# A layered convolution-attention kernel on one core: the state sum folded by transfers, d and du repeated inside SBUF, the c norm's moments on ScalarE, and new step tables

## The chip, the cores and the metric

The kernel runs on one core of a Trainium2 chip. Its engines are PE (TensorE, matrix products into PSUM), DVE (VectorE), ACT (ScalarE), POOL (GpSimd) and SP (SyncE, which here only issues transfers); 16 DMA engines move data between DRAM and SBUF, and inside SBUF. Each engine works through its own instructions in order and waits on semaphores for the others. The metric is the device time of one execution in microseconds (us): the median of three runs of the kernel before is 1173.12 us (1171.61 to 1173.38).

## The reference, cut to what matters

The input `x` is 4 images of 64 x 64 points with 96 channels, in float32: 4 x 4096 tokens of 96.

Layer 0 normalizes x over groups of 3 channels (group norm), then each token over its 96 channels (here: the c norm), projects it to `value`, `gate`, `delta` and to A, B and C of 96 channels x 16 states each, and runs a recurrence along the 4096 tokens of an image:

```python
h_new = d * (A_t * h) + d * (B_t * u_t[..., None])     # 96 channels x 16 states
y = g_t * jnp.sum(C_t * h_new, axis=-1)                # sum over the 16 states
```

`y @ W_out + b_out` is added to x. Layer 1 normalizes the tokens (the a norm), applies an attention without softmax, with 6 heads, whose products can be taken in another order (a Gram matrix of the tokens of one image, then one 97 x 96 matrix for the whole image), adds it to the tokens, normalizes again (the f norm) and adds a two-layer network with 384 hidden units, whose operands are rounded to 8 bits and whose sums are rounded to 16.

## The kernel before

**Tiles and chunks.** An image is cut into 8 chunks of 512 tokens, 32 chunks in all. The 96 x 16 states are cut into 12 tiles of 128 rows: 4 groups of 4 states (`sh`) times 3 groups of 32 channels (`cg`). One tile of one chunk is one *step* of the main loop: 384 steps, 12 to a chunk. In step s, PE makes B of tile s+3, A of tile s+1 and C of tile s, each as three matrix products that together keep float32 precision; ACT copies B from PSUM and adds its bias (`b_copy`, L888); POOL multiplies it by du (`b_mul`, L891); DVE multiplies A by d in PSUM (`a_mul`, L900), runs the recurrence over the 512 tokens as a scan (`scan`, L907), and multiplies h by C (`c_mul`, L931). In four of the twelve tiles, listed in `ON_POOL`, this last product is made by ACT and POOL in two parts (`c_copy`, L937, and `c_mul_pool`, L940). ACT keeps the last column of h for the next chunk (`keep`, L917). B has one PSUM bank, A two, C two, and three ("M") serve everything else.

**The state sum.** The products of one chunk lie in four tiles `ch` of 128 x 3 x 512, one for each `sh`. POOL issues three accumulating transfers (`gather`, L946) that add the tiles of `sh` 1, 2 and 3 to that of `sh` 0. In it, the 128 rows are four states times 32 channels. `state_sum` (L955) adds the four on PE by a product with `fold`, four stacked unit matrices, into PSUM. `gated` (L993) multiplies by the gate, and `project_out` (L998) and `residual` (L1003) follow.

**The front of a chunk** (class `Front`) runs 9 to 39 steps ahead of the chunk: load, `centre` and `scale` for the group norm on POOL (L747, L750), `stats` of the c norm on DVE, `rstd` on POOL, `apply` on ACT, the transposition, the split into two parts (`low` and three transfers of SP), and the projections for d and u. d and d*u come as `dd` of 96 x 2 x 512. Every tile needs them repeated over its four states: `write` (L824) puts `dd` into DRAM and `read` (L831) brings it back four times into `rep`, 32 rows each.

**The norms.** `LayerNorm.stats` runs `bn_stats` (L433) and `bn_aggr` (L435) on DVE, four of each. `Roots.root` then runs four small instructions on POOL: variance plus epsilon (L406), the power -1/2 (L409), the mean times -1 (L412), times the root (L413). `apply` (L450) scales and shifts on ACT.

**The order.** It is written out by hand: the table `AT` gives, for each piece of work, the step in relation to its chunk's (or its image's) first step, and `at` puts it on that step's list, which runs after the step's own instructions. So a piece's number says what it stands behind on each engine's queue, and on SP's. What does not fit into the 384 steps goes to a planner (`end`, class `Plan`) with costs and ranks, which tries 1500 random orders by its own costs and takes the best. The start, up to step 6, is planned in the same way (`planned_start`). In images 1 to 3 the loop carries the second layer of the image before as well.

Of the kernel before, what the change touches and what calls it, by code (L numbers as in the profile page):

```python
# [9 lines left out]
F32 = mybir.dt.float32  # L10
# [7 lines left out]
P = 128  # L18
# [4 lines left out]
J = 4  # L23
# [17 lines left out]

    "load_x": -39, "centre": -25, "scale": -24, "stats": -22, "rstd": -22, "apply": -21,
    "transpose": -14, "affine": -13, "upper": -13, "low": -12, "proj_d": -9, "d_out": -9,
    "proj_u": -9, "du_out": -9, "write": -9, "read": -6, "proj_gate": -3, "gate_out": -1,

    "gather1": 7, "gather2": 11, "gather3": 14,

    "state_sum": 18, "gated": 18, "project_out": 19, "residual": 19, "stats_a": 20,
    "rstd_a": 21, "apply_a": 22, "transpose_a": 33, "keep": 34, "spill": 39, "gram": 24,
    "gram_out": 24, "gram_add": 26,  # L50

    "fetch": 21, "attention": 26, "residual_f": 26, "stats_f": 26, "rstd_f": 27, "apply_f": 29,
    "transpose_f": 30, "quant_in": 31, "hidden0": 37, "relu0": 37, "hidden1": 31, "relu1": 33,
    "hidden2": 38, "relu2": 38, "project_f": 40, "round_out": 40, "bias_out": 40, "total": 46,
    "store": 51,

    "sums": -31, "sums_out": -30,
}
MV_BUFS = {1: 4, 2: 2}
END_RANKS = (-2, 0, 1)  # L60
END_PAIR = (0, 1, 1, 2, 2, 3, 3, 4)
APPLY_DVE = (0, 2, 4, 6, 7)
QUANT_POOL = (1, 4)
BIAS_DVE = (0, 1, 2, 3, 4, 5, 6, 7)
TOTAL_DVE = (1, 3, 5, 7)
ON_POOL = (0, 2, 7, 8)
XBUFS = 15
END_TRIES = 1500
# [3 lines left out]
def conv_attn_hybrid_kernel(  # L72
# [34 lines left out]
        "bu": 5, "h": 3, "cha": 2, "chb": 3,  # L107
# [97 lines left out]
    minus = const.tile([P, 3, J], F32, name="minus")  # L205
    nc.gpsimd.memset(minus, -1.0)
    eps_t = {}
    for eps, n in ((1e-3, 1), (1e-5, 2)):
        eps_t[eps] = const.tile([P, n, J], F32, name=f"eps{n}")
        nc.gpsimd.memset(eps_t[eps], eps)  # L210
# [169 lines left out]
    class Roots:  # L380
# [14 lines left out]
        def root(self, shift=True):  # L395
            if self.done:
                return
            self.done = True
            n = len(self.of)
            for k, ln in enumerate(self.of):  # L400
                if k and ln.eps == self.of[k - 1].eps:
                    continue
                m = k + 1
                while m < n and self.of[m].eps == ln.eps:
                    m += 1
                nc.gpsimd.tensor_tensor(  # L406
                    self.r[:, k:m], self.mv[:, k:m, :, 1], eps_t[ln.eps][:, 0 : m - k], ALU.add
                )
            nc.gpsimd.tensor_tensor(self.r, self.r, mhalf[:, 0:n], ALU.pow)  # L409
            if not shift:  # L410
                return
            nc.gpsimd.tensor_tensor(self.nmr, self.mv[:, :, :, 0], minus[:, 0:n], ALU.mult)  # L412
            nc.gpsimd.tensor_tensor(self.nmr, self.nmr, self.r, ALU.mult)  # L413

    class LayerNorm:
# [9 lines left out]
        def stats(self, src):  # L425
# [8 lines left out]
            for j in range(J):  # L434
                nc.vector.bn_aggr(self.mv[:, j, :], st[:, j, :])  # L435

# [3 lines left out]

        def offset(self):

            nc.vector.tensor_scalar(self.r, self.mv[:, :, 1], self.eps, None, ALU.add)

        def root(self):
            nc.gpsimd.tensor_tensor(self.r, self.r, mhalf[:, 0], ALU.pow)
# [19 lines left out]
    class Plan:  # L466
# [23 lines left out]
        def run(self, fill=None):  # L490
# [67 lines left out]
            rng = random.Random(1)  # L558
# [24 lines left out]
    steps = {}  # L583

# [151 lines left out]
    class Front:  # L736
# [15 lines left out]
        def stats(self):  # L752
            self.ln.stats(self.t)
# [53 lines left out]
        def wide_d(self, cg):  # L807
            if cg == 0:
                rep[self.b, self.i] = sb("rep", [P, 2, NCG, TC], F32, f"rep_{self.nm}")
# [782 lines left out]
```

## Time and profile before

| | before |
|---|---|
| median of three runs | 1173.12 us |
| the profiled execution's own time | 1169.27 us |
| its span | 1167.5 us |
| PE, DVE busy | 1129.6, 1116.8 us |
| POOL, ACT busy | 1008.9, 811.3 us |
| first scan, last scan start | 35.1, 1102.7 us |

A profile is of one execution. "Busy" is the time in which at least one instruction of the engine was under way; PE's ends are modelled. A row of a group has the source line, the engine, the operation, what it writes and reads, the shapes and the count, then the total busy time in us, the mean of one in ns, the idle time before them and what ended it. A row of waits has the waiting engine, line and result, what it waited for, the total in us, the times and the longest. In a row of a timeline stand the start, the duration, the engine, the line and the operation. In a row of a stretch stand the stretch, its length, busy us of PE, its weight loads, DVE, ACT and POOL (each with the number of instructions), the granted clock, the DMA share and GB/s.

### The profile page before, as it was taken

Reading aid. Unit: us, or ns where it says so; the run is one execution under the profiler, and the core shown is the slowest. Engines: PE = TensorE matmul, PEld = TensorE weight load, DVE = VectorE, ACT = ScalarE, POOL = GpSimd, SP = SyncE. Lnnn points to the kernel's source line nnn. Section 1 sums busy time; section 2 is a strip of 40 time slices with the busy share of each in tenths; the row PEclk is TensorE's granted clock in tenths of the full one; section 3 lists DMA queues with packets and bytes.
Section 4 is the critical chain, followed back from the end, with each engine's and each line's share of the span. In section 5 each row is a group of like instructions: output and inputs, shape, how many; then the busy total and the mean of one; then the engine's idle time right before and its main releaser. Section 6 shows DMA issues by size and latency. Waiting matters only on the chain. (4 is left out here: it accounts for less than half of the span.)

```text
span 1167.5 us, 19144 instructions
## 1 busy us (share of the span) xinstructions
PE 1129.6 (97%) x5868; PEld 865.4 (74%) x5868; DVE 1116.8 (96%) x2110; ACT 811.3 (69%) x1818; POOL 1008.9 (86%) x1166
## 2 busy tenths in 40 slices
PE   6999999999999999999999999999999999999984
PEld 5777776777777777777877777777777777777662
DVE  6999999999999999999999999999999999999986
ACT  4666656555556777777777777787777777776477
POOL 5798888888889899899999999999999999988643
PEclk7999999999999999999999999999999999999999
DMA  7577777787776777687777778667776876777321
GB/s 183 137 167 146 165 158 160 157 178 164 166 162 151 161 166 175 148 185 162 159 163 167 165 165 189 149 152 159 167 172 149 183 160 157 150 161 166 78 82 55
DMA packets 104289, 182.13 MB, mean 156 GB/s; under 512 B 42637, under 2 KB 50769, under 8 KB 104186
## 3 DMA queue, kind: packets, MB, share of 16 engines
q1 hardware_dynamic: 90060, 106.96, 38.9%
q0 software_dynamic: 13536, 73.93, 31.8%
q8 instruction: 46, 0.75, 0.3%
q14 instruction: 57, 0.47, 0.1%
q10 hardware_dynamic: 590, 0.02, 0.0%
HBM read 69.12 MB, written 24.77 MB: 80 GB/s over the span
## 5 line engine op out<-in xcount | busy, mean ns | idle before, releaser
L891 POOL TENSOR_TENSOR bu<-bu,rep 128x512 f32<-128x512 f32 x384 | 511.3, 1342 | 51.1 <-ACT state L917 39.7
L907 DVE TENSOR_TENSOR_SCAN h<-Aps,state,bu 128x512 f32<-128x512 f32 x336 | 426.1, 1268 | 0.3 <-issue 0.2
L888 ACT ACTIVATE bu<-Bps,b_bac 128x512 f32<-128x512 f32 x384 | 262.8, 684 | 198.7 <-PE Bps L283 190.8
L900 DVE SCALAR_TENSOR_TENSOR Aps<-Aps,b_bac,rep 128x512 f32<-128x512 f32 x384 | 281.8, 734 | 3.6 <-PE Aps L283 3.1
L283 PE MATMUL Bps<-xs,w 128*128 128x512 f32 x768 | 266.9, 429 | 3.4 <-ACT bu L888 3.1
L283 PE MATMUL Aps<-xs,w 128*128 128x512 f32 x768 | 241.7, 395 | 1.2 <-DVE h L907 1.0
L940 POOL TENSOR_TENSOR ch<-ch,h 128x512 f32<-128x512 f32 x126 | 168.1, 1334 | 9.7 <-ACT ch L937 5.1
L283 PEld LDWEIGHTS Aps<-xs,w 128*128 128x128 f32 x768 | 143.6, 188 | 37.2 <-DVE h L907 2.9
L283 PEld LDWEIGHTS Bps<-xs,w 128*128 128x128 f32 x768 | 126.5, 190 | 45.5 <-ACT gx_ps L632 12.6
L283 PE MATMUL Aps<-xl,w 128*128 128x512 f32 x384 | 151.8, 395 | 0.0
L283 PE MATMUL Bps<-xl,w 128*128 128x512 f32 x384 | 151.4, 394 | 0.0
L283 PE MATMUL Cps<-xs,w 128*128 128x512 f32 x384 | 120.6, 395 | 0.0
L283 PE MATMUL Dps<-xs,w 128*128 128x512 f32 x384 | 120.6, 395 | 0.0
L931 DVE SCALAR_TENSOR_TENSOR ch<-Dps,b_bac,h 128x512 f32<-128x512 f32 x160 | 118.6, 741 | 0.4
L946 POOL DMA_DIRECT2D ch<-ch x94 | 88.7, 944 | 2.3 <-DMA ch<-ch 1.7
L283 PEld LDWEIGHTS Aps<-xl,w 128*128 128x128 f32 x384 | 72.0, 188 | 17.8
L283 PEld LDWEIGHTS Bps<-xl,w 128*128 128x128 f32 x384 | 72.2, 188 | 17.5
L283 PEld LDWEIGHTS Cps<-xs,w 128*128 128x128 f32 x384 | 72.0, 188 | 17.6
L283 PEld LDWEIGHTS Dps<-xs,w 128*128 128x128 f32 x384 | 72.0, 188 | 17.6
L937 ACT ACTIVATE ch<-Cps,b_bac 128x512 f32<-128x512 f32 x94 | 64.5, 686 | 24.3 <-PE Cps L283 24.3
L283 PE MATMUL Cps<-xl,w 128*128 128x512 f32 x192 | 75.7, 395 | 0.0
L283 PE MATMUL Dps<-xl,w 128*128 128x512 f32 x192 | 75.6, 394 | 0.0
(203 smaller groups left out, 2013.7 us busy)
## 6 DMA issues: line engine op xcount, KB each, us to landing
ch<-ch POOLq DMA_DIRECT2D x94, 768.0 KB, 6.6
rep<-ddd SPq DMA_DIRECT2D x124, 384.0 KB, 7.3
ddd<-dd SPq DMA_DIRECT2D x31, 384.0 KB, 3.2
xl<-lo SPq DMA_DIRECT2D x62, 128.0 KB, 2.4
x<-in_x_dram SPq DMA_DIRECT2D x32, 192.0 KB, 3.0
xatd<-xat SPq DMA_DIRECT2D x32, 192.0 KB, 3.8
xal<-xatd SPq DMA_DIRECT2D x32, 192.0 KB, 3.4
out_dram<-o SPq DMA_DIRECT2D x32, 192.0 KB, 3.4
```

Of the source, the lines that this page charges most:

```text
L283: nc.tensor.matmul(ps, lhsT=wt[:, n], rhs=mv, start=(n == 0), stop=(n == 2))
L888: nc.scalar.activation(self.bu, self.b_ps, AF.Identity, bias=self.bias(0))
L891: nc.gpsimd.tensor_tensor(self.bu, self.bu, rep[self.b, self.i][:, 1, self.cg], ALU.mult)
L900: nc.vector.scalar_tensor_tensor(self.a_ps, self.a_ps, self.bias(1), rep[self.b, self.i][:, 0, self.cg], ALU.add, ALU.mult,)
L907: nc.vector.tensor_tensor_scan(self.h, self.a_ps, self.bu, 0.0 if self.i == 0 else state[self.sh, self.cg], ALU.mult, ALU.add,)
L931: nc.vector.scalar_tensor_tensor(self.slot(), self.c_ps, self.bias(2), self.h, ALU.add, ALU.mult)
L937: nc.scalar.activation(self.ch, self.c_ps, AF.Identity, bias=self.bias(2))
L940: nc.gpsimd.tensor_tensor(self.ch, self.ch, self.h, ALU.mult)
L946: nc.gpsimd.dma_start(chs[g, 0], chs.pop((g, sh)), accum_op=ALU.add)
```

## The change

- **State sum.** Except in the last chunk, `state_sum` is gone. After the three gathers POOL issues two more accumulating transfers: `halve(g, 64)` adds rows 64 to 127 to rows 0 to 63, `halve(g, 32)` rows 32 to 63 to rows 0 to 31. `collect` has SP bring the three blocks of 32 rows x 512 into `y` of 96 x 512, and `gated` reads `y` from SBUF.
- **d and du.** `rep` is laid out with d and du side by side for each channel group, and twelve transfers of SP (`spread`, four times three) copy `dd` into it inside SBUF. `write` and `read` are gone.
- **c norm.** Its moments are made on ACT, but for the first two chunks: `sums` adds up each of four blocks of 96 with an accumulator (L436 in the changed kernel) and makes the negated mean; `squares` does the same for the squares of the centred values (L444) and makes variance plus epsilon.
- **All norms.** Variance plus epsilon and the negated mean of the a and f norms are made by two small `tensor_scalar` on DVE at the end of `stats` (L426, L428). POOL is left with the power (L401) and one product (L403).
- **Tables.** `AT` has new steps throughout, `AT0` others for image 0 (`table(b)`); `ON_POOL` is (2, 4, 9, 11), `ON_POOL0` (0, 2, 9, 11), and the very last tile's product stays on DVE. The gathers stand on 8, 11 and 14, `halve` on 15 and 18, `collect` on 21, `gated` on 23. The lists that say which engine does what in the tail are new, the f norm's roots in the tail are taken one by one, and the planner makes 250 tries from another seed.

```diff
-    "proj_u": -9, "du_out": -9, "write": -9, "read": -6, "proj_gate": -3, "gate_out": -1,
-    "gather1": 7, "gather2": 11, "gather3": 14,
-    "state_sum": 18, "gated": 18, "project_out": 19, "residual": 19, "stats_a": 20,
-    "rstd_a": 21, "apply_a": 22, "transpose_a": 33, "keep": 34, "spill": 39, "gram": 24,
...
+    "load_x": -32, "centre": -28, "scale": -27, "stats": -26, "squares": -24, "rstd": -22,
+    "apply": -20, "transpose": -14, "affine": -13, "upper": -13, "low": -12, "proj_d": -10,
+    "d_out": -9, "proj_u": -8, "du_out": -8, "spread0": -7, "spread1": -7, "spread2": -7,
+    "spread3": -4, "proj_gate": 3, "gate_out": 4, "gather1": 8, "gather2": 11, "gather3": 14,
+    "halve64": 15, "halve32": 18, "collect": 21, "state_sum": 22, "gated": 23,
+    "project_out": 24, "residual": 24, "stats_a": 26, "rstd_a": 26, "apply_a": 27,
...
-END_PAIR = (0, 1, 1, 2, 2, 3, 3, 4)
-APPLY_DVE = (0, 2, 4, 6, 7)
-QUANT_POOL = (1, 4)
-BIAS_DVE = (0, 1, 2, 3, 4, 5, 6, 7)
-TOTAL_DVE = (1, 3, 5, 7)
-ON_POOL = (0, 2, 7, 8)
+END_PAIR = (0, 1, 2, 3, 4, 5, 6, 7)
+APPLY_DVE = (1, 2, 6)
+QUANT_POOL = (0, 1, 2, 3, 5, 7)
+BIAS_DVE = (0, 2, 4, 5, 6, 7)
+TOTAL_DVE = (1, 3, 4, 5, 6)
+ON_POOL = (2, 4, 9, 11)
...
+    "proj_u": -9, "du_out": -9, "spread0": -7, "spread1": -7, "spread2": -7,
...
+    "project_out": 24, "residual": 24, "stats_a": 24, "rstd_a": 25, "apply_a": 27,
...
+ON_POOL0 = (0, 2, 9, 11)
...
-                nc.gpsimd.tensor_tensor(
-                    self.r[:, k:m], self.mv[:, k:m, :, 1], eps_t[ln.eps][:, 0 : m - k], ALU.add
-                )
-            nc.gpsimd.tensor_tensor(self.r, self.r, mhalf[:, 0:n], ALU.pow)
-            if not shift:
-                return
-            nc.gpsimd.tensor_tensor(self.nmr, self.mv[:, :, :, 0], minus[:, 0:n], ALU.mult)
-            nc.gpsimd.tensor_tensor(self.nmr, self.nmr, self.r, ALU.mult)
+            nc.gpsimd.tensor_tensor(self.r, self.r, mhalf[:, 0 : len(self.of)], ALU.pow)
+            if shift:
+                nc.gpsimd.tensor_tensor(self.nmr, self.nmr, self.r, ALU.mult)
...
             for j in range(J):
                 nc.vector.bn_aggr(self.mv[:, j, :], st[:, j, :])
+            nc.vector.tensor_scalar(self.r, self.mv[:, :, 1], self.eps, None, ALU.add)
+            if shift:
+                nc.vector.tensor_scalar(self.nmr, self.mv[:, :, 0], -1.0, None, ALU.mult)
+
+        def sums(self, src):
+            self.group = Roots()
+            self.group.of.append(self)
+            self.group.tiles()
+            t = small.tile([P, J], F32, tag="lns", name=f"lns_{self.nm}", bufs=2)
+            for j in range(J):
+                nc.scalar.activation(
+                    src[:, j, :], src[:, j, :], AF.Identity, accum_out=t[:, j : j + 1]
+                )
+            nc.scalar.activation(self.nmr, t, AF.Copy, scale=-1.0 / C)
+
+        def squares(self, src):
+            t = small.tile([P, J], F32, tag="lnq", name=f"lnq_{self.nm}", bufs=2)
+            for j in range(J):
+                nc.scalar.activation(
+                    junk, src[:, j, :], AF.Square, bias=self.nmr[:, j : j + 1],
+                    accum_out=t[:, j : j + 1],
+                )
+            nc.scalar.activation(self.r, t, AF.Identity, scale=1.0 / C, bias=eps_c)
...
-        def write(self):
-            self.dr = dram.tile([2, C, TC], F32, tag="dd", name=f"ddd_{self.nm}", bufs=3)
-            nc.sync.dma_start(self.dr.rearrange("k p n -> p k n"), self.dd)
-
-        def read(self):
-
-            src = self.dr.rearrange("k (g c) n -> c (k g) n", c=32)
-            t = rep[self.b, self.i].rearrange("p k g n -> p (k g) n")
-            for q in range(4):
-                nc.sync.dma_start(t[q * 32 : (q + 1) * 32], src)
+        def spread(self, q):
+            t, dd = rep[self.b, self.i], self.dd
+            for cg in range(NCG):
+                nc.sync.dma_start(
+                    t[q * 32 : (q + 1) * 32, cg], dd[cg * 32 : (cg + 1) * 32]
+                )
...
+    def halve(g, n):
+        t = chs[g, 0]
+        nc.gpsimd.dma_start(t[0:n], t[n : 2 * n], accum_op=ALU.add)
+
+    y_sb = {}
+
+    def collect(g):
+        t, y = chs.pop((g, 0)), sb("y", [C, TC], F32, f"y_{g}")
+        for cg in range(NCG):
+            nc.sync.dma_start(y[cg * 32 : (cg + 1) * 32], t[0:32, cg])
+        y_sb[g] = y
...
         def gated():
-            nc.vector.tensor_tensor(yg[0:C, :], y_ps.pop(g), gate.pop((b, i)), ALU.mult)
+            y = y_sb.pop(g) if g in y_sb else y_ps.pop(g)
+            nc.vector.tensor_tensor(yg[0:C, :], y, gate.pop((b, i)), ALU.mult)
...
-            (("state_sum", state_sum, g), ("gated", gated)),
+            (("gated", gated),) if g < N - 1 else (("state_sum", state_sum, g), ("gated", gated)),
```

## The prediction

> **What bounds the kernel now.** I read the page's busy shares first, then busy time by stretches of 100 us, then the groups by line, then the waits, and last the timeline of single steps. One chunk is 12 tiles; the starts of the scans in the timeline give one chunk per 33.5 us between 771 and 1073 us (302 us for nine), and about 32 us in image 0. Columns: PE, weight loads, DVE, ACT, POOL; one row of image 0 and two of image 2.
>
> ```profile
> 200.00:300.00 100.00, 99.31 (x484) 77.14 (x483) 98.56 (x166) 59.86 (x139) 88.82 (x99) 1.00 0.77 162
> 800.00:900.00 100.00, 100.00 (x526) 77.08 (x525) 98.13 (x186) 73.95 (x159) 93.46 (x106) 1.00 0.76 164
> 900.00:1000.00 100.00, 100.00 (x521) 77.06 (x520) 98.42 (x184) 74.88 (x171) 93.63 (x108) 1.00 0.74 164
> ```
>
> DVE is at 98%, PE reads 100% (its ends are modelled, so that is no proof), POOL at 93.5% and ACT at 75%. Per chunk of 33.5 us: DVE 32.9, POOL 31.4, ACT 24.9. DVE's missing 0.6 us has a name in the waits (engine, line, waited for: us, times, longest):
>
> ```profile
> DVE x L1003 <- PE o_ps L998: 17.2, 29, 1.0
> POOL bu L891 <- ACT state L917: 39.7, 56, 1.4
> ```
>
> 17.2 us over 29 chunks is 0.6 us each: DVE stands until `project_out` is through PE. It doesn't wait for POOL, which waits itself (second line). So DVE sets the pace, PE a close second. The rows that the change touches:
>
> ```profile
> L433 DVE BATCH_NORM_STATS2 st_c<-z 128x6 f32<-128x96 f32 x128 | 23.2, 242 | 0.0
> L435 DVE BATCH_NORM_AGGREGATE mv_c<-st_c 128x2 f32<-128x6 f32 x128 | 11.5, 150 | 0.0
> L993 DVE TENSOR_TENSOR yg<-y_ps,gate 96x512 f32<-96x512 f32 x32 | 21.8, 681 | 1.9 <-PE y_ps L955 1.9
> L406 POOL TENSOR_TENSOR rstd_c<-mv_c,eps 128x4 f32<-128x4 f32 x31 | 6.5, 209 | 26.4 <-DVE mv_c L435 24.8 <-DVE gm L660 1.6
> L412 POOL TENSOR_TENSOR nmr_c<-mv_c,minus 128x4 f32<-128x4 f32 x31 | 6.0, 192 | 0.0
> L946 POOL DMA_DIRECT2D ch<-ch x94 | 88.7, 944 | 2.3 <-DMA ch<-ch 1.7 <-POOL bu L891 0.6
> L632 ACT ACTIVATE gx_ps<-gx_ps,gmc 96x512 f32<-96x512 f32 x24 | 15.6, 650 | 0.0
> L632 ACT ACTIVATION_READ_ACCUMULATOR gx_ps<-gx_ps,gmc 96x1 f32 x24 | 4.6, 194 | 0.0
> ```
>
> And the two places where a small DVE instruction meets POOL, from the timeline (start, duration):
>
> ```profile
> 450.61 1.27 POOL L891 TENSOR_TENSOR bu<-bu,rep 128x512 f32<-128x512 f32 x1 [0.57 <-ACT state L917]
> 451.61 0.29 DVE L640 TENSOR_SCALAR gt<-gt 96x2 f32<-96x2 f32 x1
> ...
> 1160.27 0.91 POOL L1236 TENSOR_TENSOR o<-x,yb 128x384 f32<-128x384 f32 x1 [6.40 <-DVE yb L1230]
> 1160.51 1.08 DVE L1230 TENSOR_TENSOR yb<-y,b_q 128x384 f16<-128x384 f16 x1 [0.32 <-ACT y L1226]
> ```
>
> The 2-element `tensor_scalar` ends at 451.90, just after POOL's product at 451.88; L443, of the same kind with POOL idle, took 169 ns. The second took 1.08 where its like take 0.56: it ran after POOL's sum had ended at 1161.18.
>
> **What the skill says.** The Trainium skill, "SBUF — State Buffer", section "Who interferes with whom": a DVE `tensor_scalar` with source and result in SBUF can take a two-port mode and then locks GpSimd's ports, and a DVE instruction with two SBUF inputs contends with a GpSimd instruction that reads SBUF; the later one blocks fully. The four lines above agree (0.29 for 0.17, 1.08 for 0.56). "DMA: Bandwidth & Descriptors", section "Anatomy of one DMA — SWDGE (gpsimd) path": about 2.0 us + bytes / 436e3; for the 768 KB gather that is 3.8 us, the page's issue list has 6.6, so I scale by 1.7. "ScalarE: Activation LUTs", section "What ACT_TABLE_LOAD costs": 0.833 ns an element, which I use to bring the 512-element rows down to 96; no run here shows a 96-element accumulation.
>
> **The change, part by part, per chunk.**
>
> *State sum.* Off PE: six matmul records, 0.99 us from the first to the next instruction in the timeline. PE needs at most 33.5 - 1.0 = 32.5. In their place POOL issues `halve64` and `halve32`: 2 x 0.944 = 1.89 us if the issue costs what 128 rows cost, 0.71 if it goes with the rows (96/128 of one). I take 1.89. SP issues three `collect` transfers. The chain must be there for `gated` at step 23. From the third gather's issue: POOL's order puts its 0.94, three powers and three products (3 x 1.25), one `bu` and one `ch` (2.7) ahead of `halve64`, 7.4 us, and the gather has landed by 6.6; then `bu`, `bu`, `ch`, `bu` and the issue, 6.3 us, against a landing of (2.0 + 0.9) x 1.7 = 4.9; `halve32` lands in about 4.2 more; three issues at 0.5 (four took 2.00 for `rep`) and 2.7 to land: 22.1 us. Nine steps of 2.79 are 25.1. So it is hidden by 3 us; behind `yg` stands all of DVE, so every us over that is lost in full.
>
> *`gated`.* `y` now comes from SBUF, so `yg` has two SBUF inputs and waits for POOL's running product. POOL is in a 1.3 us product most of the time: mean wait 0.5 (0 to 1.3). The read itself stays 0.68. +0.5 on DVE.
>
> *`project_out`.* Between `yg` and `x` DVE now has a scan, a product, mostly a `ch`, and `lo`, 3.3 us against 1.9 before, so PE's answer is there: -0.6 in images 1 to 3 (0.3 in image 0), bounds -0.7 to 0. Next to be late is the `collect` above.
>
> *c norm's moments.* Off DVE: four statistics and four aggregates, 0.92 us in the timeline from the first to the next instruction (the busy sums overlap). On to ACT: rows of 650 and 574 less 416 x 0.833 = 303 and 227; 4 x (227 + 190) + 4 x (303 + 194) + 2 x 203 = 4.1 us. ACT goes to 29.0 of 33, 88%, in blocks of about 2 us. `bu` copies queue behind them and PE's only B bank behind those; in before ACT waits for Bps 190.8 us in all, so this is covered, but thinly (uncovered: up to 0.5 a chunk). POOL's wait for mv_c goes.
>
> *Offset and negated mean, a and f norms.* +2 `tensor_scalar` of 128x4 each on DVE. The first is like L443, starting after a 35 ns gap where others overlap by 80, so 0.20; the second 0.09: 0.29 a norm, 0.58 a chunk (0.29 in image 0, which has no f norm). POOL loses 3 x (0.21 + 0.19) = 1.2 (0.8 in image 0). Both new instructions can wait for POOL. In images 1 to 3 the a, f and c roots stand in one step, and POOL's order there is the third gather, then powers and small products alone. At mv_c in before POOL has always finished the gather and is waiting for DVE, and DVE instructions of this kind beside a power keep their length (L457 at 0.32 with L409 under way). So I take 0 there (bounds 0 and 4 x 1.3). In image 0 `stats_a` is two steps earlier, beside `bu` and `ch`: two waits, 0.5 in all.
>
> *d, du.* Twelve transfers in SBUF instead of one write and four reads through DRAM: SP issues 6 us instead of 2.3, in a queue with tens of us of slack; rep is needed at step -2, nine transfers are issued from -7 and three from -4, and 128 KB SBUF to SBUF landed in 2.4 to 3.0. Hidden; a late one would stop POOL, then DVE. DMA load: the write goes, the halves add (64 + 32)/384 of the gathers' 31.8% share, 8%, so 0.75 becomes about 0.8.
>
> *Tail and start.* In the last 57 us ACT is busy 43, and the chain that ended last is mostly ACT `h`, `hq` and `xn`. Four quantizations (1.54 each) go from ACT to POOL, two applies (1.5) come to ACT: -3 of ACT. Chunk 30's `project_out` now falls to the tail, about +1. Net -2 (-6 to +3). Start: 0 (two for one queue order, +-1).
>
> **The sum.** Images 1 to 3, DVE: -0.92 - 0.6 + 0.5 + 0.58 = -0.44, to 33.06. POOL: 31.4 + 1.9 - 1.2 = 32.1, below it by 1; PE 32.5, ACT 29.0: DVE still sets the pace. 23 chunks x 0.44 = 10. Image 0: -0.92 - 0.3 + 0.5 + 0.29 + 0.5 = +0.1, eight chunks, +1. Tail -2. In all -11 to -12: span 1167.5 to 1156. The profiled execution took 1169.27, 1.8 around its span, and lies 3.85 below the median of 1173.12; I take the same difference off the median: **1161.5 us**.
>
> **Rivals.** *POOL takes over.* POOL's 32.1 has only 1 us of play, and it has never run above 94% here. If its waits for `bu` copies, held up by ACT's new blocks, stay at the 1.4 us a chunk that it has now, chunks take 33.5 and only the tail is gained: 1171. For: four engines above 88%. Against: POOL's waits now are mostly for DVE and ACT at places where it is ahead.
>
> *Slower: the small `tensor_scalar`s meet POOL's products.* Place: the four new DVE instructions after the aggregates, one after the other on the bounding engine. If POOL lags by one product, each pair waits 0.65 for the running product and as much again if POOL's next product gets in between. One wait per norm: -0.44 + 1.3 = +0.9 x 23 = 20, with image 0 +5 and the tail -2: 1196. Two per norm: 1226. It decides from 0.11 us per instruction (0.44 / 4) on.
>
> *Faster: PE was the bound.* If PE's 100% is real, DVE's stalls go with the 0.99 and waits for the lock overlap with what was idle: 0.9 x 31 + 3 = 31, so 1142. For: PE's digits; against: DVE's 98%.
>
> **How the numbers follow.** Forecast 0.50 (own range 1152 to 1169); POOL takes over 0.14, half of it within 0.2%; slower by the lock 0.24; PE bound 0.12. 0.2% is 2.3 us, about what a measurement of this kernel can tell from no change. Faster: 0.48 + 0.12 + 0.04 = 0.64; same 0.08; slower 0.28. The range 1142 to 1194 leaves out the lock's upper half and what is beyond PE's 1142.
>
> **What would show it.** Right: `yg` near 1.1 to 1.2 us mean; `x` no longer waiting for o_ps; rows of `rstd_a` and `nmr_a` on DVE near 0.17 in images 1 to 3 and longer in image 0; DVE still at 98%, POOL 96 to 97%, ACT near 88% in the middle; no wait of DVE for `y`'s transfer. Wrong: the small rows at 0.6 or more (lock), POOL waiting for its own gathers or DVE for `bu` (POOL bound), chunks of 32.6 or less (PE), or `yg` waiting for a DMA.

## The result, and the profile after

The changed kernel takes 1339.5 us in the median of 4 runs (1319.9 to 1349.2), the kernel before 1173.0. Two of the four runs, 1349.2 and the profiled one of 1343.9, are slow ones (over 1.5% above the fastest), so the ratio of 1.132, with a 95% interval of 1.129 to 1.136, and every difference from the changed kernel below rest on the other two, 1319.9 and 1335.1, whose mean is 1327.5. The forecast was 1161.5 us, its range ended at 1194. The change makes the kernel slower by 155 us; as those two runs lie 15 us apart, differences from it are good to about 8 us. Most of the loss comes by a mechanism that the prediction named but priced at an eighth of its size.

First the busy time in the three stretches that were shown of before.

```profile
200.00:300.00 100.00, 88.46 (x405) 69.60 (x404) 96.00 (x128) 62.61 (x186) 82.36 (x82) 0.95 0.77 157
800.00:900.00 100.00, 90.01 (x446) 70.31 (x445) 94.64 (x160) 74.24 (x199) 82.48 (x89) 0.93 0.70 146
900.00:1000.00 100.00, 87.57 (x422) 67.51 (x421) 93.27 (x136) 71.15 (x184) 84.35 (x83) 0.95 0.76 157
```

TensorE, DVE and POOL all do less in 100 us than before (POOL 82 against 93), ScalarE is at 63 to 74, and TensorE's granted clock has dropped from 1.00 to 0.93 to 0.95. So no engine has been given more work than it can do. Nor is all of DVE's 94% work, as its rows show:

```profile
L1017 DVE TENSOR_TENSOR yg<-y,gate 96x512 f32<-96x512 f32 x31 | 145.4, 4690 | 28.8 <-DMA y<-ch 28.8
L426 DVE TENSOR_SCALAR rstd_a<-mv_a 128x4 f32<-128x4 f32 x32 | 6.5, 204 | 1.1
L428 DVE TENSOR_SCALAR nmr_a<-mv_a 128x4 f32<-128x4 f32 x32 | 5.2, 162 | 0.0
L961 POOL DMA_DIRECT2D ch<-ch x62 | 59.0, 952 | 13.4 <-DMA ch<-ch 12.2 <-issue 1.1
```

`yg`, 681 ns before, is 4690 ns in the mean. That is 31 x 4.01 = 124 us, and DVE waits 28.8 us more for `y`. The waits say who stands behind it:

```profile
PE o_ps L1022 <- DVE yg L1017: 122.7, 27, 6.1
POOL bu L902 <- ACT state L928: 81.1, 28, 4.8
POOL rstd_a L401 <- DVE nmr_a L428: 80.1, 26, 7.1
DVE yg L1017 <- DMA y<-ch: 28.8, 25, 2.6
DVE x L1027 <- PE o_ps L1022: 2.1, 1, 2.1
```

TensorE waits for `yg`, and GpSimd, which looks like the victim in the second and third line, waits for what comes after `yg` on DVE. One `yg` of the timeline shows what happens in its 6.7 us:

```profile
554.76 0.89 POOL L957 DMA_DIRECT2D ch<-ch  x1
554.96 6.72 DVE L1017 TENSOR_TENSOR yg<-y,gate 96x512 f32<-96x512 f32 x1
555.38 1.23 POOL L1252 TENSOR_TENSOR yb<-y,b_q 128x384 f16<-128x384 f16 x1
556.27 1.57 POOL L902 TENSOR_TENSOR bu<-bu,rep 128x512 f32<-128x512 f32 x1
557.51 1.54 POOL L951 TENSOR_TENSOR ch<-ch,h 128x512 f32<-128x512 f32 x1
558.73 1.18 POOL L1258 TENSOR_TENSOR o<-x,yb 128x384 f32<-128x384 f32 x1
559.60 1.53 POOL L902 TENSOR_TENSOR bu<-bu,rep 128x512 f32<-128x512 f32 x1
```

GpSimd does five more products, the last of which ends at 561.13. `yg` ends at 561.68, 0.55 us later: it ran only when GpSimd had stopped. And GpSimd stopped because its next `bu` waited, by way of ScalarE, for DVE. Two details mattered later: the gather's issue just ahead of the products, and that each product's record starts before the last one's has ended (556.27 against 556.61).

An account of the two profiled executions, 1342.1 against 1167.5 us of span (+174.6): from the first scan to the last it is +166.6, the stretch after the last scan 72.0 against 64.8 (+7.2), the start +0.8. Of the 166.6, `yg`'s length and its wait for `y` make 153, if none of it covered other waits.

### The profile page after: what moved, and what is told of

It is laid out like the page before. It is cut to its first block, busy times and chain, and to the rows that moved or that the text cites. A ratio compares the mean times of both kernels' runs of the same rounds, so it can differ in the third digit from the quotient of the medians.

```text
span 1342.1 us, 20031 instructions
## 1 busy us (share of the span) xinstructions
PE 1178.8 (88%) x5683; PEld 914.9 (68%) x5683; DVE 1239.8 (92%) x1988; ACT 901.6 (67%) x2363; POOL 1037.9 (77%) x1055
## 5 line engine op out<-in xcount | busy, mean ns | idle before, releaser
L902 POOL TENSOR_TENSOR bu<-bu,rep 128x512 f32<-128x512 f32 x384 | 572.6, 1540 | 119.3 <-ACT state L928 81.1
L285 PE MATMUL Bps<-xs,w 128*128 128x512 f32 x768 | 277.3, 443 | 4.4 <-ACT bu L899 2.5
L285 PE MATMUL Aps<-xs,w 128*128 128x512 f32 x768 | 252.4, 411 | 3.7 <-DVE h L918 3.4
L951 POOL TENSOR_TENSOR ch<-ch,h 128x512 f32<-128x512 f32 x125 | 183.5, 1468 | 16.0 <-issue 9.4
L1017 DVE TENSOR_TENSOR yg<-y,gate 96x512 f32<-96x512 f32 x31 | 145.4, 4690 | 28.8 <-DMA y<-ch 28.8
L1022 PE MATMUL o_ps<-w_o,yg 97*128 97x96 f32 x256 | 57.5, 397 | 123.2 <-DVE yg L1017 122.7
L1022 PEld LDWEIGHTS o_ps<-w_o,yg 97*128 97x128 f32 x256 | 50.5, 293 | 135.1 <-DVE yg L1017 113.1
L942 DVE SCALAR_TENSOR_TENSOR ch<-Dps,b_bac,h 128x512 f32<-128x512 f32 x129 | 95.7, 742 | 6.9 <-PE Dps L285 6.7
L942 DVE SCALAR_TENSOR_TENSOR ch<-Cps,b_bac,h 128x512 f32<-128x512 f32 x130 | 96.0, 739 | 0.0
L401 POOL TENSOR_TENSOR rstd_a<-rstd_a,mhalf 128x4 f32<-128x4 f32 x32 | 32.6, 1019 | 80.3 <-DVE nmr_a L428 80.1
```

The costliest lines, as they stand in the source:

```text
L285: nc.tensor.matmul(ps, lhsT=wt[:, n], rhs=mv, start=(n == 0), stop=(n == 2))
L401: nc.gpsimd.tensor_tensor(self.r, self.r, mhalf[:, 0 : len(self.of)], ALU.pow)
L902: nc.gpsimd.tensor_tensor(self.bu, self.bu, rep[self.b, self.i][:, self.cg, 1], ALU.mult)
L942: nc.vector.scalar_tensor_tensor(self.slot(), self.c_ps, self.bias(2), self.h, ALU.add, ALU.mult)
L951: nc.gpsimd.tensor_tensor(self.ch, self.ch, self.h, ALU.mult)
L1017: nc.vector.tensor_tensor(yg[0:C, :], y, gate.pop((b, i)), ALU.mult)
```

## The experiments

"The ports" are in the following those that a DVE instruction with two SBUF inputs and a GpSimd instruction can't use at once (the prediction's "lock"). GpSimd "keeps" them if its next product runs although DVE's instruction is ready; otherwise DVE "gets" them. A "train" or "run" is a row of GpSimd products that stand ready one behind the other. The theory at the start: `yg` waits for a whole run of GpSimd's products, and with `y`'s late landing that makes the 153 us. The rivals: one product's length at most, as predicted, and the loss comes from the transfers; or the tables, ScalarE's moments and the small `tensor_scalar`s cost most.

### The lock by itself (micro)

```diff
+ nc.gpsimd.tensor_tensor(flag, res, src2, ALU.mult)
+ for k in range(6):
+     nc.gpsimd.tensor_tensor(t[k], src, src2, ALU.mult)      # train; chain: t[0] <- t[0]
+ nc.vector.tensor_tensor(res[0:96], flag[0:96], src2[0:96], ALU.mult)
```

> This kernel leaves the whole computation out (the output is a copy of x). It measures the lock by itself: one DVE instruction becomes ready while GpSimd has nothing to do, runs six independent 128x512 products (a train), or runs six products each of which needs the one before (a chain). The DVE instruction is a 96x512 product of two SBUF tiles, the same with one input in PSUM, a scalar_tensor_tensor of two SBUF tiles, a 128x96 tensor_scalar, or a 128x4 tensor_scalar. Theory A (GpSimd keeps the ports for a whole train, since it issues the next product before the last one has ended): the two-SBUF product takes about 0.7 us alone, about 0.7 + 6 x 1.25 = 7 to 8 us against the train, and about 0.7 + 1.3 = 2 us or less against the chain; the PSUM form 0.7 everywhere. Theory B (one product's length, as the prediction had it): 2 us or less against both. Theory C (the length of yg in the changed kernel is not a matter of the ports): 0.7 us against all three.

Measured: 0.69 us alone, 1.73 against the train and 1.73 against the chain; scalar_tensor_tensor the same; 0.69 everywhere with one input in PSUM; the 128x96 `tensor_scalar` 0.21, 1.25 and 1.25, the 128x4 one 0.17, 1.21 and 1.21. Theory B held: DVE gets the ports after one product. My theory fell in this form.

### The state sum undone (sum_pe), and the lock put into the kernel before (y_copied)

```diff
-                at(s0 + table(b)["halve64"], halve, g, 64)
-                at(s0 + table(b)["halve32"], halve, g, 32)
-                at(s0 + table(b)["collect"], collect, g)
...
-            (("gated", gated),) if g < N - 1 else (("state_sum", state_sum, g), ("gated", gated)),
+            (("state_sum", state_sum, g), ("gated", gated)),
```

> The changed kernel with the state sum on TensorE again (no halves, no collect; yg reads PSUM at the same step), all else as changed. Theory A (the yg product's lock and the late y are the loss: 31 x 4.0 + 28.8 = 153 us): yg back at 0.68 us and 1170 to 1200 us. Rival (the new tables, ScalarE's moments or the small tensor_scalars cost most of it): above 1260 us, with yg at 0.68 us all the same.

Measured: 1185.7 us (ratio to before 1.013, 1.008 to 1.018), `yg` 677 ns. So the state sum's part of the change costs about 142 us of the 155; all the rest together costs about 13.

```diff
+        def y_copy():
+            y_sb[g] = sb("y", [C, TC], F32, f"y_{g}")
+            nc.scalar.copy(y_sb[g], y_ps.pop(g))
...
-    "state_sum": 18, "gated": 18, "project_out": 19, "residual": 19,
+    "state_sum": 18, "y_copy": 18, "gated": 19, "project_out": 20, "residual": 20,
```

> The kernel before, with one thing added: ScalarE copies y from PSUM to SBUF, and yg (one step later) reads the copy, so that it has two SBUF inputs. No transfers, no new tables. Theory A (a whole train of GpSimd's products is waited for): yg at 2.5 to 5 us in the mean and 1240 to 1300 us. Theory B (one product): yg at 1.1 to 1.4 us and 1180 to 1205 us. Rival (the halves, collect and their lateness make the loss): below 1195 us whatever yg's length.

Measured: 1177.2 us (1.0034, 1.0024 to 1.0045), and `yg` with its two SBUF inputs:

```profile
L997 DVE TENSOR_TENSOR yg<-y,gate 96x512 f32<-96x512 f32 x31 | 35.6, 1148 | 0.0
```

1148 ns is what the prediction had said (1.1 to 1.2). The time came out below theory B's 1180 to 1205: 31 x 0.47 = 14 us more of `yg` cost only 4 us, so not every us of DVE is lost in this kernel (more on that below). And two SBUF inputs against a busy GpSimd are not enough for 4.7 us. Here is what GpSimd has in hand at one of these `yg`:

```profile
555.60 0.88 POOL L946 DMA_DIRECT2D ch<-ch  x1
556.64 1.28 POOL L891 TENSOR_TENSOR bu<-bu,rep 128x512 f32<-128x512 f32 x1 [0.16 <-ACT bu L888]
557.23 1.24 DVE L997 TENSOR_TENSOR yg<-y,gate 96x512 f32<-96x512 f32 x1
558.03 1.59 POOL L940 TENSOR_TENSOR ch<-ch,h 128x512 f32<-128x512 f32 x1
```

It is so at all 31: one product is under way, and the next, `ch`, starts 0.08 us after ScalarE's copy that it needs (here 557.95). So GpSimd has no second product ready when the first ends, where in the `yg` shown above it had four more. A gather's issue stands ahead here as well, 1.3 to 2.9 us before each `yg`: an issue alone doesn't make `yg` long.

### Without DVE in it (yg_pool)

```diff
-            nc.vector.tensor_tensor(yg[0:C, :], y, gate.pop((b, i)), ALU.mult)
+            engine = nc.gpsimd if g < N - 1 else nc.vector
+            engine.tensor_tensor(yg[0:C, :], y, gate.pop((b, i)), ALU.mult)
```

> The changed kernel with yg computed by GpSimd instead of DVE in chunks 0 to 30; halves, collect and tables stay. GpSimd gets 1.0 us a chunk more and now waits itself for y's transfer. Theory A (DVE's stall in the lock is the main loss): 1190 to 1260 us, DVE without waits for y. Rival (the transfers' lateness and GpSimd's added issues are the main loss): above 1290 us.

Measured: 1234.8 us (1.051, 1.048 to 1.055). Taking the product off DVE gives about 93 us back, as theory A had it, and DVE has no wait for `y`; now its `x` waits 55.9 us for o_ps.

### A DMA issue ahead of the products (micro_issue)

In the trace of the changed kernel, GpSimd's records overlap by over 0.2 us in some 105 runs, and all of these begin right behind a DMA issue (a gather or a half). During `yg`'s waits in it, at 86 product ends the next record had started over 0.25 us earlier: at 85 of them GpSimd kept the ports. At the 27 with 0.13 us or less (or a gap) DVE got them, 27 times. In y_copied no product end within a wait of `yg` had the overlap, and DVE got the ports every time. (How a wait is counted at its ends moves these counts by one to three.)

```diff
+ nc.gpsimd.dma_start(moved, given, accum_op=ALU.add)         # or a plain copy, or nothing
  six products; DVE's instruction needs the first of them
```

> This kernel leaves the whole computation out (the output is not the reference's). One DVE instruction becomes ready when the first of six GpSimd products ends; ahead of the six stands either nothing or a DMA issue on GpSimd (accumulating, or a plain copy). Theory D (after a DMA issue GpSimd runs its instructions 0.3 us ahead, so that the next product stands at the ports before the last one ends, and DVE gets them only when GpSimd runs out of ready work): the two-SBUF product takes 1.7 us without an issue and 6 to 7 us behind either issue; against a chain of products that each need the one before it stays at 1.7 us even behind an issue, and the PSUM form at 0.7 us; the 128x96 tensor_scalar 1.25 us without an issue and 5 to 7 us behind one. Rival (the length of yg in the changed kernel has another cause, such as y's transfers): 1.7 us everywhere for the product.

The timeline of this kernel:

```profile
8.96 1.73 DVE L43 TENSOR_TENSOR res<-t,src 96x512 f32<-96x512 f32 x1 [1.50 <-POOL t L62]
16.64 0.97 POOL L55 DMA_DIRECT2D moved<-given  x1
17.37 7.60 POOL L62 TENSOR_TENSOR t<-src,src 128x512 f32<-128x512 f32 x6
18.94 6.59 DVE L43 TENSOR_TENSOR res<-t,src 96x512 f32<-96x512 f32 x1 [8.25 <-POOL t L62]
28.74 6.59 DVE L43 TENSOR_TENSOR res<-t,src 96x512 f32<-96x512 f32 x1 [3.21 <-POOL t L62]
38.79 1.74 DVE L43 TENSOR_TENSOR res<-t,src 96x512 f32<-96x512 f32 x1 [3.46 <-POOL t L65]
49.02 0.69 DVE L46 TENSOR_TENSOR res<-p_in,t 96x512 f32<-96x512 f32 x1 [8.49 <-POOL t L62]
57.52 6.11 DVE L49 TENSOR_SCALAR res<-t 128x96 f32<-128x96 f32 x1 [7.81 <-POOL t L62]
67.10 6.11 DVE L49 TENSOR_SCALAR res<-t 128x96 f32<-128x96 f32 x1 [3.48 <-POOL t L62]
```

The first line has no issue ahead of the products: 1.73. Behind an accumulating issue (18.94) and behind a plain copy (28.74) the same instruction takes 6.59 us: it waits for all the products that are left. Against a chain behind an issue (38.79) it is 1.74 again, with a PSUM input (49.02) 0.69. The `tensor_scalar`s behave like the product. The one at 57.52 was meant to have no issue ahead and missed its expectation (1.25): GpSimd had not stopped since the issue at 46.83, so it still kept the ports. So the effect that theory D forecast is shown here: behind an issue the ports are kept over a run of ready products. Its mechanism is not. How far ahead the records start is not what counts: behind the copy they overlap by only 0.03 to 0.06 us, as in the first block, and the ports are kept. Nor does a first issue change GpSimd for the rest of the program: in y_copied gathers are issued throughout, and `yg` never waited for more than the product under way.

### In the real kernel: gather_early, pool_yields, yields_later

```diff
-    "spread3": -4, "proj_gate": 3, "gate_out": 4, "gather1": 8, "gather2": 11, "gather3": 14,
+    "spread3": -4, "proj_gate": 3, "gate_out": 4, "gather1": 6, "gather2": 9, "gather3": 14,
```

> The changed kernel with the first two gathers of each chunk issued earlier (steps 6 and 9 instead of 7 or 8 and 10 or 11), so that the second gather of the next chunk no longer stands in the step just ahead of yg. Theory D: yg's mean falls from 4.7 to 1.0 to 1.8 us and the time to 1210 to 1265 us (about 100 of the 124 us go, DVE's wait for y's transfer stays). Rival (any train of GpSimd's products holds DVE here, or it is the transfers): yg stays at 4 us or more and the time above 1310 us.

Measured: 1444.2 us (1.230, 1.228 to 1.232). Theory D's forecast missed, and by its numbers the rival's held:

```profile
L1017 DVE TENSOR_TENSOR yg<-y,gate 96x512 f32<-96x512 f32 x31 | 215.9, 6965 | 46.8 <-DMA y<-ch 46.8
```

In images 1 to 3 a gather still stood ahead of `yg`, and now eight or nine products followed it without a break: most of `yg`s there took 9 to 11 us. In image 0, where none stood there, `yg` fell to 1.2 us in the mean of chunks 2 to 8 (4.3 in the changed kernel), but DVE's wait for `y` grew from 7.2 to 21.7 us (100 to 370 us of the span), and the chunks took as long as in the changed kernel. So moving an issue moves the stall, which the rival doesn't account for; but the time of image 0 didn't follow, with the late `y` right behind.

```diff
             nc.vector.tensor_tensor(yg[0:C, :], y, gate.pop((b, i)), ALU.mult)
+            if g < N - 1:
+                nc.gpsimd.tensor_copy(one, yg[0:1, 0:1])
```

> The changed kernel with a one-element copy of yg on GpSimd, put behind the work that GpSimd has ahead of it in step 23, so that GpSimd's run of products ends there and waits for yg. Theory D: yg's mean falls to 1.0 to 2.5 us and the time to 1220 to 1290 us, though GpSimd now waits for y's transfer too. Rival (the length of yg has nothing to do with how long GpSimd keeps on): yg stays at 4 us or more and the time above 1330 us.

Measured: 1223.6 us (1.041, 1.038 to 1.044), as theory D had it.

```profile
L1018 DVE TENSOR_TENSOR yg<-y,gate 96x512 f32<-96x512 f32 x31 | 49.9, 1611 | 28.6 <-DMA y<-ch 28.6
```

Making GpSimd stop for `yg` takes about 104 us off the changed kernel. This is the direct test on the kernel itself: same transfers, same tables, same instruction on DVE, and the wait for `y` is as long as it was (28.6 against 28.8 us). Of the state sum's 142 us, 38 are left.

```diff
  pool_yields, and in both tables (in image 0 "stats_a" and "rstd_a" go to 26 too):
-    "gated": 23, "project_out": 24, "residual": 24
+    "gated": 25, "project_out": 26, "residual": 26
```

> pool_yields with yg, the output projection and the residual two steps later (25, 26 and 26), so that y has landed. If the run of products behind a DMA issue and the late y are all that the state sum's move costs (1185.7 in sum_pe, 1223.6 in pool_yields, where DVE waits 28.6 us for y and yg takes 1.1 us more than in sum_pe 31 times), the wait for y goes to under 5 us and the time to 1190 to 1207 us. Rival (GpSimd's two added issues and its stop cost as much again): 1215 us or more.

Measured: 1221.7 us (1.043, 1.040 to 1.045); DVE waits 0.5 us for `y` instead of 28.6, and the time doesn't move, as the rival had it. My accounting, in which waits add up, failed: `yg` got longer (1928 ns), DVE waits 20.7 us for o_ps, ScalarE 39.9 for `nmr_a`.

### Breaking the run without waiting: issue_reset, reset_24

```diff
+    def settle():
+        nc.gpsimd.memset(pair[:, 0:1], 1.0)
+        nc.gpsimd.tensor_copy(pair[:, 1:2], pair[:, 0:1])
...
         nc.gpsimd.dma_start(chs[g, 0], chs.pop((g, sh)), accum_op=ALU.add)
+        settle()
```

> The changed kernel with two one-element operations on GpSimd behind each gather's and each half's issue, the second of which needs the first. Nothing in it waits for yg or y. Theory (a product behind a DMA issue keeps the ports until GpSimd first has to wait, and a dependent pair is such a wait): yg's mean falls to 1.0 to 2.0 us and the time to 1205 to 1235 us, though GpSimd gets about 2 us of work more a chunk. Rival (only a stop for work of another engine ends the run): yg stays above 3.5 us and the time above 1310 us.

Measured: 1207.7 us (1.029, 1.027 to 1.031), `yg` 821 ns, as the theory wanted. But then `yg` one step later (in image 0 the statistics and the root too):

```diff
-    "gated": 23, "project_out": 24, "residual": 24, "stats_a": 26
+    "gated": 24, "project_out": 25, "residual": 25, "stats_a": 26
```

> issue_reset with yg one step later (24; projection and residual 25), and the statistics and root in image 0 one step later with them; in images 1 to 3 the statistics stay at 26, so that the root is not pushed onto GpSimd's way as in yields_later, settled and y_raised. Theory (DVE's wait for y, 34.4 us in issue_reset, is on the path): the wait goes and the time falls to 1172 to 1190 us. Rival (it covers other work, TensorE's or GpSimd's, that is late as well): 1198 us or more with the wait for y gone all the same.

Measured: 1311.0 us (1.119, 1.116 to 1.121). By its numbers the rival held, but not for its reason:

```profile
L1025 DVE TENSOR_TENSOR yg<-y,gate 96x512 f32<-96x512 f32 x31 | 116.0, 3742 | 0.6 <-DMA y<-ch 0.6
```

The wait for `y` is gone and the long `yg` is back. The timelines show the difference: in issue_reset `yg` became ready at an issue or just ahead of one, in the pair, or in the first product behind it, and got the ports there. In reset_24 it mostly became ready two products or more behind a pair, and then in all but a few cases waited until GpSimd's next issue, three to five products on. So the pair is no cure. It brings the overlap from 0.3 down to 0.03 us, yet the ports are kept all the same at some 70% of the product ends during `yg`'s waits. In these runs the keeping ended where GpSimd waited for another engine, at its next DMA issue, and at each link of a chain; why products behind the pair are kept again stays open.

### The other parts of the change: moments_alone, moments_pieces, spread_alone

```diff
-    "stats": -22, "rstd": -22, "apply": -21,
+    "stats": -23, "squares": -22, "rstd": -21, "apply": -20,
...
-("stats", f.stats), ("rstd", f.ln.rstd),
+("stats", f.sums), ("squares", f.squares), ("rstd", f.ln.rstd),
```

> The kernel before with the c norm's moments on ScalarE alone (accumulating activations, the root one step later, apply one step later); a and f norms, state sum, d/du and tables as before. The prediction's term (DVE -0.92 us a chunk, ScalarE's 4.1 us covered): 31 chunks, 1145 to 1165 us. Rival (ScalarE's blocks hold up the bu copies, and these TensorE's only B bank; seen in sum_pe, where TensorE waits 17.6 us for nmr_c): 1172 to 1195 us, with TensorE waiting for ScalarE's moments.

Measured: 1203.9 us (1.026, 1.025 to 1.028), even above the rival's range. Three of its waits:

```profile
POOL ch L974 <- ACT ch L971: 71.5, 36, 3.5
PEld Bps L286 <- ACT bu L922: 45.8, 33, 2.1
DVE dd L824 <- ACT dd L820: 34.5, 27, 1.7
```

In before the first was 5.1 us, the second 9.9, and the third not there. ScalarE is busy 78 to 83 us of 100 and yet late: the four sums take 1.4 us in a row, the squares 2.3, with a quantization of about 2.0 us between them and another behind.

```diff
-    "stats": -23, "squares": -22, "rstd": -21, "apply": -20,
+    "sum0": -25, "sum1": -24, "sum2": -23, "sum3": -22, "square0": -21, "square1": -20,
+    "square2": -19, "square3": -18, "rstd": -17, "apply": -15,
```

> moments_alone with the c norm's accumulations on ScalarE one a step, over eight steps (centre and scale two steps earlier, root and apply four steps later), instead of four in each of two steps. ScalarE's work is the same. Theory (blocks of about 2 us beside other blocks hold up the bu copies, and through TensorE's one B bank the whole pipe): 1160 to 1185 us. Rival (ScalarE's total of 4.1 us more a chunk is what counts): 1195 us or more.

Measured: 1179.1 us (1.006, 1.004 to 1.008). The same work in pieces costs 6 us instead of 30, as the theory had it. The blocks were most of the loss, not the total of ScalarE's work; the edit also puts `centre` and `scale` two steps earlier and the root and `apply` four and five later, which this run doesn't part from the pieces. And DVE, relieved of 0.92 us a chunk, gave nothing in return.

```diff
-            for q in range(4):
-                nc.sync.dma_start(t[q * 32 : (q + 1) * 32], src)
+            for cg in range(NCG):
+                nc.sync.dma_start(t[q * 32 : (q + 1) * 32, cg], dd[cg * 32 : (cg + 1) * 32])
```

> The kernel before with d and du repeated by twelve transfers inside SBUF instead of a write to DRAM and four reads; all else as before. The prediction's term (hidden): 1168 to 1178 us. Rival (twelve issues on SP and more load on the DMA engines make rep or a gather late): 1182 us or more, with DVE or GpSimd waiting for rep.

Measured: 1172.9 us (1.0005, 0.9992 to 1.0018). Hidden, as predicted.

### What bounds the kernel before: residual_later, pe_relief, both_relief

```diff
-    "project_out": 19, "residual": 19,
+    "project_out": 19, "residual": 20,
```

> The kernel before with only the residual one step later (20 instead of 19), so that DVE has other work while TensorE does the output projection. The prediction priced this wait at 0.6 us a chunk of DVE. If DVE sets the pace: DVE's 17.2 us wait for o_ps goes and the time falls by 10 to 17 us, to 1155 to 1164 us. Rival (another engine is as close, and DVE waits elsewhere for as long; y_copied, in which this wait was gone too, stood 0.3% above before): 1168 to 1176 us.

Measured: 1173.2 us (1.001, 1.000 to 1.002). DVE's wait for o_ps is gone, and another has its size (the same line of before stands first):

```profile
DVE Aps L900 <- PE Aps L283: 3.1, 6, 0.9
DVE Aps L900 <- PE Aps L283: 17.0, 33, 1.0
```

DVE waits for TensorE at another place for as long. That fits a TensorE that is late and not badly ordered; the next run tests it.

```diff
+        if last is None:
+            nc.tensor.matmul(y_ps[g], lhsT=ones16[:, 0:C], rhs=ones16, start=True, stop=True)
+            return
         for cg in range(NCG):
```

> The kernel before with the state sum's matmuls of chunks 0 to 30 left out: one bf16 matmul of constants (about 0.2 us) stands in their place, so that y is a constant there and the output is not the reference's. TensorE gets about 0.8 us a chunk less, DVE, GpSimd and the transfers nothing less. If DVE sets the pace (the prediction): 1168 to 1176 us. If TensorE is as close (the prediction's third rival; in residual_later DVE's wait for o_ps came back as 17.0 us of waiting for Aps): 1150 to 1167 us.

Measured: 1148.6 us (0.980, 0.978 to 0.981): 24 us for 31 x 0.8 us of TensorE (0.8 is the expectation's estimate). (The tiles of `ch` also come free without waiting for the matmuls here, which this run doesn't part from the relief.)

```profile
800.00:900.00 100.00, 100.00 (x523) 78.74 (x522) 99.90 (x190) 76.15 (x167) 95.82 (x110) 1.00 0.76 165
```

DVE goes from 98.1 to 99.9%, its wait for o_ps from 17.2 to 1.6 us, and a chunk takes 32.9 us: exactly DVE's work of 32.9 us in the prediction. TensorE reads 100% before and after, so its digits couldn't have told.

> pe_relief with the residual one step later as in residual_later: the same constant in the place of the state sum. If DVE and TensorE limit each other, the two reliefs together give more than the sum of each (0 alone for the residual): 1145 to 1160 us, and below pe_relief by 5 us or more. Rival (GpSimd, at 93%, sets the pace): no lower than 1166 us and GpSimd's share at 95% or more.

Its edit is pe_relief's and residual_later's together. Measured: 1157.7 us (0.987, 0.986 to 0.989). It was to be 5 us below pe_relief and is 9 above. The time was in the expected range, the order of the two wasn't. With TensorE in time, a later residual has no wait to save (1.6 us of it were left); through what the 9 us come is not settled.

### Putting the gain together: settled, y_raised

```diff
  settled: issue_reset, "gated": 25, "project_out": 26, "residual": 26, and sums and squares one a step
  y_raised: the changed kernel with the same steps and pieces, no settle(), and
+        def raise_y():
+            y_ps[g] = bank("M", [C, TC], f"y_ps_{g}")
+            nc.scalar.copy(y_ps[g], y_sb.pop(g))
```

> issue_reset with yg two steps later (25; projection and residual 26) and the c norm's accumulations on ScalarE one a step: the three costs found, taken away together, while TensorE stays free of the state sum (worth 24 us in pe_relief). If they are all of the loss: from 1207.7 about 34 us of DVE's wait for y and about 10 to 20 us of ScalarE's blocks go, to 1150 to 1175 us. Rival (GpSimd, at 95% in issue_reset, is the limit now, or ends of these waits turn up elsewhere as in yields_later): 1185 us or more.

> The changed kernel with y copied by ScalarE from SBUF into a PSUM bank (step 24) before yg reads it (25), so that yg has one SBUF input and can't meet GpSimd at the ports; no added operation on GpSimd; the c norm's accumulations one a step. The halves, collect and everything else stay. If the ports, the late y and ScalarE's blocks were all of the loss: yg at 0.68 us and 1145 to 1175 us, at or below the kernel before. Rival (GpSimd's added issues, the transfers or ScalarE's load are the limit): 1185 us or more.

Measured: settled 1253.6 us (1.071, 1.067 to 1.075), `yg` 2379 ns; y_raised 1233.9 us (1.053, 1.050 to 1.056), `yg` 677 ns and 0.6 us of waiting for `y`. In both the rival's side held. y_raised says that neither the ports nor `y`'s landing explain its own 63 us above before; GpSimd waits 108.6 us for `nmr_a` (100.8 in settled), where the statistics and their root stand right behind the residual, in its step, and TensorE 66.9 for `bu` copies. DVE itself waits 44.3 us for o_ps and 24.1 for Aps (17.2 and 3.1 in before), so it waits for TensorE again. Which of these is the fourth cost was not tested alone. No version here that computes the reference beats the kernel before.

## Why the prediction was wrong, step by step

*`gated`* is the step that failed: "waits for POOL's running product: +0.5 (0 to 1.3)". The mechanism was right (two SBUF inputs meet GpSimd's reads), and where it stood alone the size was right too (y_copied: 1148 ns); but GpSimd had only one product ready at that place, which the prediction had not asked for, so that agreement is in part luck. In the changed kernel it was +4.01 us x 31. The upper bound of one product was taken from two lines in which GpSimd's run happened to end or had no DMA issue ahead. The Trainium skill, "SBUF — State Buffer", section "Who interferes with whom", gives the pair "for the whole instruction" to whoever issues first. micro agrees (1.73 = 0.69 + the rest of one product), micro_issue doesn't (6.59): behind a DMA issue the measured unit is the run of ready products, not the instruction.

*The chain third gather to `y`*, 22.1 of 25.1 us: it missed by up to 2.6 us, 25 times. In the median `yg` started 28.2 us after the third gather's issue. `halve64` was issued after 9.9 us instead of 7.4, `halve32` 5.6 later (6.3), the first transfer of `y` 5.7 later (landing priced at 4.2), and SP's three issues took 4.3 instead of 1.5. The 64 KB transfers landed after 5.9 us in the median, not 2.7 (one of that size, `xs`, already took 3.0 in before; the 2.4 was of 128 KB). The halves' issues were priced right (952 ns for 944). "Every us over that is lost in full" didn't come true: in yields_later the wait went and the time stayed.

*"DVE sets the pace, PE a close second"* was wrong for the kernel before, and with it the sum. The rival *PE was the bound* had the better reading: 0.8 us off TensorE gave 24 us (pe_relief), 0.6 and 0.9 us off DVE gave nothing (residual_later, moments_pieces). The 17.2 us that DVE waited for o_ps were read as a matter of order; they were TensorE's lateness. (For *POOL takes over* the prediction took the 1.4 us a chunk that GpSimd waits as waits for `bu` copies. The line is `keep`, L917; for `bu` copies it was 10.7 us in all.) So *`project_out`*, -0.6, came true as a wait (2.1 us are left), and in residual_later such a wait was worth nothing. The change does take the state sum off TensorE, but `yg` cost many times that gain.

*c norm's moments*: the 4.1 us of ScalarE were priced about right (sums 1.4 and squares 2.3 us in the timeline, the two small ones with them; a row of 96 took 273 and 377 ns for the 227 and 303 worked out, but the records overlap), "covered, but thinly" was wrong: 30 us alone (1.0 a chunk, where 0.5 was the bound). Mostly the blocks did it, not the share of 88%.

*Offset and negated mean*: right. 204 and 162 ns in the mean, overlapping by 0.08; only three of the a norm's 32 were over 0.3 us. The slower rival that rested on them had the right mechanism at the wrong instruction.

*d, du*: right (1.0005). *Tail*: -2 predicted, +7.2 in the profiled executions, and sum_pe has the same 71.9 us behind its last scan; which of the new tables does it was not tried.

## What to carry to other kernels

Before an operand moves from PSUM to SBUF, ask which DVE instructions then have two SBUF inputs, and what stands ahead of GpSimd's products at that moment: a DMA issue there can turn a wait of one product into a wait for everything that GpSimd has ready, and where it has only one product ready (y_copied) the wait stays short. An engine that waits for another a little, everywhere, is a sign of a limit in the other; before you remove the wait, relieve that engine in an experiment and see whether the time follows. And a block of small instructions on an engine with room to spare can cost more than its length if the engine feeds others in turn: cut it into pieces first.

## What the runs showed of the hardware that I had not expected

- A DVE product of two SBUF tiles waits for one GpSimd product (1.73 us) in a fresh run of independent products, and for the rest of the run (6.59 us for five products) when a DMA issue of GpSimd, accumulating or plain, stands ahead of it. A `tensor_scalar` of 128x96 does the same (1.25 and 6.11).
- A chain of GpSimd products, each needing the one before, hands the ports over after one, even behind an issue (1.74 us). A dependent pair of one-element operations behind the issue doesn't free the products after it (reset_24: 3.7 us in the mean).
- Behind an accumulating issue, records of GpSimd's products start about 0.3 us before the last one's end (0.26 to 0.34 in micro_issue), until GpSimd waits for something.
- In the changed kernel, where TensorE stands idle for `yg`, its granted clock was 0.93 to 0.95 in the three stretches (1.00 before), and the output projection's matmuls took 397 ns in the mean where they took 271 before: about 435 ns behind most waits of 3.7 us or more, 280 to 285 where TensorE had waited under 0.8 us.
